# Router products with the gate's weights stationary, in four column strips of the array, and a transpose back

## Chip, core and metric

The kernel runs on one core of a Trainium2 chip. The metric is the device time of one execution in microseconds (us). Engines are called PE (TensorE, products), PEld (TensorE's loads of the stationary operand), DVE (VectorE), ACT (ScalarE), POOL (GpSimd) and SP (SyncE, which issues most DMAs).

## What is computed

A "macaron" layer over x of shape 8 x 1024 x 128 in fp32: half a mixture-of-experts FFN, a causal attention, and the same half FFN once more, each over a layer norm of x.

```python
x = x + 0.5 * ffn(layernorm(x))
x = x + attention(layernorm(x))        # rotary, causal, one head of 128
x = x + 0.5 * ffn(layernorm(x))

def ffn(x):                            # xt: tokens x 128; 16 experts of 64 units, top 4
    scores = sigmoid(xt @ gate_w.T)
    _, idx = top_k(scores + gate_b, 4)
    w = take_along_axis(scores, idx)
    w = 2.5 * w / sum(w)
    comb = zeros(T, 16).at[arange(T)[:, None], idx].add(w)
    for e in range(16):
        h = silu_and_mul(xt @ w13[e].T)
        y = y + comb[:, e:e+1] * (h @ w2[e].T)
    return y + silu_and_mul(xt @ w13_s.T) @ w2_s.T
```

The change concerns the first line of the FFN only: the product of the tokens with the gate, 128 x 16.

## The kernel before

Tokens are handled in groups of 512 (`W`), four tiles (`GT`) of 128. There are eight batches of two groups, and two FFN layers: 32 groups in all, in one list with a hand-made order in which layer 1 of a batch follows its layer 0 at a distance of four batches. Group p of the list is *period* p of the program. Its main work, on PE, is: one shared up product (`up_shared`, L254), then eight steps `up(k)`, each with a gate product (L264) and an up product (L265) of 128 x 512, then nine steps `down(k)` (L276). ACT makes the silu of each up step (L267), DVE the product with it (L269), POOL the product with the routing weight `cb` (L270).

All other work is hung between these steps. A period has the slots U0 to U8 (after `up_shared` and after each up step) and D0 to D8 (after each down step). `at(p, slot, f)` puts a function into a slot, and `run` calls those of a slot in the order in which they were put there. The engines' queues are in order and follow this program order; nothing is rescheduled afterwards (`manual_schedule`). In a slot the attention's functions come first, then those of `Heads`, then those of the router, then `add` and the statistics.

The router of group p is a chain of nine functions, most of them in period p-2:

- `norm_a` (U5), `norm_b` (D1): deviation and normed tokens `xn`
- `turn` (D4): four transposes on PE (L164), one copy by ACT (L165) into `hT`, 128 x 512, which has the features on the partitions
- `route` (D6): four products (L188), a tile of `hT` stationary (128 x 128), the gate `gw` (128 x 16) streaming, so that tokens come out on partitions
- `score` (D7): ACT's exponent of the logits in PSUM (L194)
- `top_a`, `top_b` (D8), then `top_c` (period p-1, U1): the top four and their weights on DVE (L198 to L226)
- `spread` (period p-1, U3): a transpose of the weights (L235), a copy (L237), one DMA out to DRAM and four DMAs that spread them over `cb`

Group 1 has slots of its own in period 0, and group 0 runs its chain at once, before period 0.

The attention puts up to three queries into a period. The first has its exponent in D0, its transposes in D3 and D5, and its `attend` (products with V, L395, and DVE's update of x, L399) in D7; the second has its exponent in D5, its transposes in D8 and in U0 of the next period; the third has its scores in D4 and its exponent in D7. Scores are L356, the exponent is L367, the transposes are L383, their copies L387 (ACT) or L389 (DVE).

PSUM has eight banks of 512 fp32. Banks 6 and 7 are shared by all small PE work and are handed out in turn by `other_bank()`: a user waits until the reader of the use before last is through.

In fp32, a product takes two instructions on PE, each with its own load; a transpose takes one. The program orders them as load, product, load, product.

Of the kernel before, what the change touches and what calls it, by code (L numbers as in the profile page):

```python
# [9 lines left out]
F32 = mybir.dt.float32  # L10
AF = mybir.ActivationFunctionType
# [4 lines left out]
P = 128  # L16
# [10 lines left out]
def kernel(  # L27
# [14 lines left out]
    nc = tc.nc  # L42

    B, S, D = x.shape
    E = gate_w.shape[1]
    I = w_sh_down.shape[0]
    NT = S // P
    GT = 4
# [7 lines left out]
    const = ctx.enter_context(tc.tile_pool(name="const", bufs=1))  # L56
    xpool = ctx.enter_context(tc.tile_pool(name="xpool", bufs=5))
    ln = ctx.enter_context(tc.tile_pool(name="ln", bufs=2))
    small = ctx.enter_context(tc.tile_pool(name="small", bufs=3))
# [8 lines left out]
    def bank(i, n=1):  # L68
        return psum[:, i * W : (i + n) * W]
# [3 lines left out]
    def other_bank():  # L73
        spare[0] += 1
        return bank(6 + spare[0] % 2)
# [4 lines left out]
    ident = const.tile([P, P], F32, name="ident")  # L80
# [16 lines left out]
    def load_x(b, g):  # L97
        if g == 0:
            xs[b] = xpool.tile([P, NT, D], F32, tag="x", name=f"x{b}")
        tiles = slice(g * GT, (g + 1) * GT)  # L100
        nc.sync.dma_start(
            out=xs[b][:, tiles, :], in_=x[b].rearrange("(t p) d -> p t d", p=P)[:, tiles, :]
        )

    load_x(0, 0)
    gw = const.tile([P, E], F32, name="gw")
    nc.scalar.dma_start(out=gw, in_=gate_w)
    gb = const.tile([P, E], F32, name="gb")
    nc.scalar.dma_start(out=gb, in_=gate_b.broadcast_to([P, E]))
    ws = const.tile([P, 2 * I], F32, name="ws")  # L110
# [24 lines left out]
    def stats(key, b, tiles):  # L135

        if key not in mvs:
            mvs[key] = small.tile([P, NT, 2], F32, tag="mv", name=f"mv_{key}", bufs=16)
        for t in tiles:
            st = small.tile([P, 6], F32, tag="st", name=f"st_{key}_{t}")  # L140
            nc.vector.bn_stats(st, xs[b][:, t, :])
            nc.vector.bn_aggr(mvs[key][:, t, :], st)
# [26 lines left out]
    class Group:  # L169
# [12 lines left out]
            self.hT = ln.tile([P, W], F32, tag="hT", name=f"hT_{self.nm}")  # L182
            transposed(self.key, self.g, self.xn, self.hT)

        def route(self):
            self.lg = other_bank()[:, : GT * E].rearrange("p (j e) -> p j e", e=E)
            for j in range(GT):
                nc.tensor.matmul(  # L188
                    self.lg[:, j, :], self.hT[:, j * P : (j + 1) * P], gw, start=True, stop=True
                )  # L190

        def score(self):
            self.sc = small.tile([P, GT, E], F32, tag="sc", name=f"sc_{self.nm}")
            nc.scalar.activation(self.sc, self.lg, AF.Exp, scale=-1.0)  # L194

        def top_a(self):

# [221 lines left out]
    def at(p, slot, *fs):  # L419
        jobs.setdefault((p, slot), []).extend(fs)  # L420
# [3 lines left out]
    def when(p, slot):  # L424
        return p * len(slots) + slots.index(slot)
# [6 lines left out]
    for p in range(3, 29):  # L432
        for n in range(2 if p in (15, 21) or (p % 2 == 0 and p != 26) else 3):
            if not queue:
# [4 lines left out]
            s, first, e, t0, t1, a = (  # L439
                ((p, "U7"), 4, (p, "D0"), (p, "D3"), (p, "D5"), (p, "D7")),  # L440
                ((p, "D2"), 2, (p, "D5"), (p, "D8"), (p + 1, "U0"), (p + 1, "U2")),
                ((p, "D4"), 4, (p, "D7"), (p + 1, "U3"), (p + 1, "U4"), (p + 1, "U5")),
            )[n]
# [10 lines left out]
    for b in range(B):  # L454
        h, st = heads[b], starts[b]
        ready = when(turn_of[0, b, 1] + 1, "U7")
        if b == 0:
            p0, p1 = st - 1, st - 1
            places = ("U8", "D0", "D2", "D3", "D5", "D6", "D7", "D8")
        else:  # L460
            p0, p1 = st - 2, st - 1
            places = ("D0", "D3", "D5", "D8", "U1", "U3", "U4", "U6")
# [13 lines left out]

    for p, gr in enumerate(groups):
        steps = (
            gr.norm_a, gr.norm_b, gr.turn, gr.route, gr.score, gr.top_a, gr.top_b, gr.top_c,
            gr.spread,  # L480
        )
        if p == 1:
            places = [(0, s) for s in ("U1", "U2", "U5", "U6", "D0", "D1", "D2", "D3", "D4")]
        else:
            places = [(p - 2, s) for s in ("U5", "D1", "D4", "D6", "D7", "D8", "D8")]
            places += [(p - 1, "U1"), (p - 1, "U3")]
        if p > 0:
            for f, place in zip(steps, places):
                at(*place, f)
        if gr.layer == 1:  # L490
            for t in range(gr.g * GT, (gr.g + 1) * GT):
                assert done[gr.b, t] < when(p - 2, "U5")

        at(p + 1, "U3", gr.add)
        if gr.layer == 0:
            t = gr.g * GT
            for s in ("U5", "U7"):
                at(p + 1, s, lambda b=gr.b, t=t: stats(f"a{b}", b, (t, t + 1)))
                t += 2


    for b in range(2, B):
        p = turn_of[0, b, 0]
# [17 lines left out]
    gr = groups[0]  # L521
# [1 line left out]
    gr.norm_a()  # L523
    gr.norm_b()
    gr.turn()
    gr.route()
    gr.score()
    gr.top_a()
    gr.top_b()
# [90 lines left out]
```

## Time and profile before

| what | value |
|---|---|
| time, median of 3 runs (lowest, highest) | 1028.06 us (1027.17, 1028.55) |
| the profiled execution's own time | 1027.84 us |
| its span, from the first to the last instruction | 1025.7 us |
| mean granted PE clock | 0.997 |
| ACT's exponent of the logits (L194), 32 of them | mean 223 ns |
| DVE's copy of yT (L279), 32 of them | mean 682 ns |

The profile is one execution, taken by the hardware profiler. A row of a group gives line, engine, operation, names (out <- in), shapes and count, then the busy time in us and the mean of one in ns, then the engine's idle time just before such instructions and what ended it. A row of the timeline gives start and length in us; "x4" stands for four instructions in a row, merged, so that its length runs from the start of the first to the end of the last. Products are pipelined and their ends are modelled, so what a product costs PE is read from one start to the next, not from its length.

### The profile page before, as it was taken

What the parts mean: (1) busy time and instruction counts of PE and PEld (TensorE: products, weight loads), DVE (VectorE), ACT (ScalarE), POOL (GpSimd) and SP (SyncE); (2) the same over time, 40 slices, a digit from 0 to 9 for tenths busy, and PEclk for the clock granted to TensorE, in tenths of its full rate; (3) what the DMA queues carried; (4) which work ended last, traced back from release to release, by engine and by line L of the source; (5) the groups of instructions that cost most, each with busy time, mean ns of one, the idle gap of its engine ahead of it and who ended that gap; (6) DMA issues with size and microseconds to landing.
All of it is one profiled execution on the core that took longest, in us unless ns stands there. A gap on an engine that the chain in (4) does not pass through costs nothing.

```text
span 1025.7 us, 11327 instructions
## 1 busy us (share of the span) xinstructions
PE 993.1 (97%) x3520; PEld 534.2 (52%) x3520; DVE 662.5 (65%) x2032; ACT 419.7 (41%) x734; POOL 451.9 (44%) x382
## 2 busy tenths in 40 slices
PE   5799999999999999999999999999999999999997
PEld 2344455554555455545555555555565555555543
DVE  3566877667775776667677665776657757665542
ACT  2233544443534454434444444443444444343321
POOL 1445734265425562345524464334643355322433
PEclk9999999999999999999999999999999999999999
DMA  5485431354214530345213451234412343124440
GB/s 143 110 173 105 84 67 32 69 104 84 46 39 94 115 81 6 81 94 114 61 23 84 94 114 43 43 82 94 94 42 57 69 94 83 48 58 94 94 93 21
DMA packets 56748, 80.20 MB, mean 78 GB/s; under 512 B 3504, under 2 KB 23280, under 8 KB 56560
## 3 DMA queue, kind: packets, MB, share of 16 engines
q1 hardware_dynamic: 55680, 78.36, 35.5%
q10 hardware_dynamic: 1008, 1.13, 0.3%
q8 instruction: 27, 0.44, 0.2%
q14 instruction: 33, 0.27, 0.1%
HBM read 74.24 MB, written 5.24 MB: 77 GB/s over the span
## 4 chain that ended last, share of the span: by engine, by line
PE 86%; DVE 7%; DMA 2%; issue 2%; ACT 2%; POOL 0%; SPq 0%; ACTq 0%; POOLq 0%; DVEq 0%
PE psum L276 23%; PE psum L265 18%; PE psum L264 17%; PE psum L356 6%; PE psum L395 6%; PE psum L383 3%; PE psum L323 3%; PE psum L188 3%; PE psum L164 2%; PE psum L254 2%; DVE hidT L269 1%; DMA cb<-cd 1%; PE psum L337 1%; DVE sel L220 1%; PE psum L284 1%
## 5 line engine op out<-in xcount | busy, mean ns | idle before, releaser
L270 POOL TENSOR_TENSOR hidT<-hidT,cb 128x512 f32<-128x512 f32 x256 | 324.0, 1270 | 545.2 <-DVE hidT L269 497.3
L265 PE MATMUL psum<-hT,wu 128*128 128x512 f32 x512 | 263.2, 596 | 4.4 <-DVE hidT L269 4.4
L264 PE MATMUL psum<-hT,wg 128*128 128x512 f32 x512 | 263.4, 596 | 0.0
L267 ACT ACTIVATE sg<-psum 128x512 f32<-128x512 f32 x256 | 152.7, 597 | 233.0 <-PE psum L264 217.5
L276 PE MATMUL psum<-hidT,wd 128*128 128x512 f32 x512 | 248.0, 598 | 0.0
L269 DVE TENSOR_TENSOR hidT<-psum,sg 128x512 f32<-128x512 f32 x256 | 175.2, 686 | 100.5 <-PE psum L265 98.4
L265 PEld LDWEIGHTS psum<-hT,wu 128*128 128x128 f32 x512 | 97.7, 191 | 128.2 <-issue 104.2
L276 PEld LDWEIGHTS psum<-hidT,wd 128*128 128x128 f32 x512 | 89.2, 191 | 69.0 <-issue 62.7
L264 PEld LDWEIGHTS psum<-hT,wg 128*128 128x128 f32 x512 | 89.4, 193 | 65.8 <-issue 62.8
L387 ACT COPY prT<-psum 128x512 f32<-128x512 f32 (+2 forms) x64 | 32.4, 506 | 158.6 <-PE psum L383 158.6
L395 PEld LDWEIGHTS psum<-v,prT 128*128 128x128 f32 x576 | 74.4, 192 | 30.6 <-issue 26.5
L395 PE MATMUL psum<-v,prT 128*128 128x128 f32 x576 | 74.6, 275 | 0.0
L356 PE MATMUL psum<-k,q 128*128 128x512 f32 (+2 forms) x192 | 72.4, 486 | 0.0
L399 DVE SCALAR_TENSOR_TENSOR x<-psum,rl,x 128x128 f32<-128x128 f32 x64 | 22.1, 346 | 77.1 <-PE psum L395 70.0
L155 DVE TENSOR_SCALAR xn_f<-x,mv_f,rs_f 128x128 f32<-128x128 f32 x128 | 65.6, 573 | 5.8 <-POOL rs_f L148 5.7
L383 PEld LDWEIGHTS psum<-ident,pr 128*128 128x128 f32 x288 | 36.8, 141 | 49.9 <-issue 42.9
L356 PEld LDWEIGHTS psum<-k,q 128*128 128x128 f32 x192 | 36.6, 190 | 45.8 <-issue 45.1
L362 DVE TENSOR_REDUCE top<-psum 128x1 f32<-128x128 f32 (+3 forms) x64 | 48.5, 758 | 2.2
L383 PE MATMUL psum<-ident,pr 128*128 128x128 f32 x288 | 47.4, 274 | 1.9 <-DVE x L287 1.9
L367 ACT ACTIVATE pr<-psum,top 128x128 f32<-128x128 f32 (+3 forms) x64 | 47.3, 743 | 0.3
L360 DVE TENSOR_TENSOR psum<-psum,causal 128x128 f32<-128x128 f32 x64 | 19.0, 296 | 42.4 <-PE psum L356 42.0
L256 ACT ACT_TABLE_LOAD x31 | 39.8, 1283 | 10.2 <-PE psum L254 10.1
(77 smaller groups left out, 1013.6 us busy)
## 6 DMA issues: line engine op xcount, KB each, us to landing
cb<-cd SPq DMA_DIRECT2D x128, 512.0 KB, 8.5
x<-in_x SPq DMA_DIRECT2D x16, 256.0 KB, 10.9
out_x<-x SPq DMA_DIRECT2D x16, 256.0 KB, 2.4
cd<-cT SPq DMA_DIRECT2D x32, 32.0 KB, 1.8
cs<-in_rope SPq DMA_DIRECT2D x1, 1024.0 KB, 12.4
wd<-in_w_down SPq DMA_DIRECT2D x1, 512.0 KB, 8.1
wg<-in_w_gate ACTq DMA_DIRECT2D x2, 256.0 KB, 7.5
wu<-in_w_up ACTq DMA_DIRECT2D x2, 256.0 KB, 6.4
```

Source lines behind the costliest of these rows:

```text
L155: nc.vector.tensor_scalar(xn[:, j, :], xs[b][:, t, :], mvs[key][:, t, 0:1], rstd[:, j : j + 1], ALU.subtract, ALU.mult,)
L264: nc.tensor.matmul(g_ps, wg[:, units], self.hT, start=True, stop=True)
L265: nc.tensor.matmul(u_ps, wu[:, units], self.hT, start=True, stop=True)
L267: nc.scalar.activation(sg, g_ps, AF.Silu)
L269: nc.vector.tensor_tensor(hid, u_ps, sg, ALU.mult)
L270: nc.gpsimd.tensor_tensor(hid, hid, self.cb[:, k, :], ALU.mult)
L276: nc.tensor.matmul(self.y, w, h, start=(k == 0), stop=(k == NP))
L356: nc.tensor.matmul(s[:, c:e], h.q[:, i * P : width], h.k[:, c:e], start=True, stop=True)
L362: nc.vector.tensor_reduce(top, s[:, :width], AX.X, ALU.max)
L367: nc.scalar.activation(self.pr[:, : self.width], self.s[:, : self.width], AF.Exp, bias=self.top, scale=SCALE, accum_out=self.h.rl[:, self. ...
L383: nc.tensor.transpose(tp[:, j, :], self.pr[:, (k + j) * P : (k + j + 1) * P], ident)
L395: nc.tensor.matmul(o, self.prT[:, j, :], self.h.v[:, j, :], start=(j == 0), stop=(j == i))
```

## The change

The gate's weights become the stationary operand. `gw` is widened from 16 to 32 columns (`SW`), with zeros in the columns from 16 on, and each of the four token tiles gets a product of its own with it, in its own strip of 32 columns of the array: tile j writes partitions 32 j to 32 j + 31 of one 128 x 128 piece of PSUM. The logits now have experts on the partitions and tokens on the columns. ACT copies this piece to SBUF (`lt`), PE transposes it, and the exponent reads the 16 valid columns of each strip from the transposed piece.

`route` thereby becomes two functions, and one slot is used differently: `route_a` (products and copy) stands in D5, `route_b` (the transpose) in D7, ahead of `score`, which stays in D7. In period 0, for group 1, they stand in U6 and U8. Group 0 calls them one after the other.

```diff
-    gw = const.tile([P, E], F32, name="gw")
-    nc.scalar.dma_start(out=gw, in_=gate_w)
+    SW = P // GT
+    gw = const.tile([P, SW], F32, name="gw")
+    nc.vector.memset(gw[:, E:], 0.0)
+    nc.scalar.dma_start(out=gw[:, :E], in_=gate_w)
...
-        def route(self):
-            self.lg = other_bank()[:, : GT * E].rearrange("p (j e) -> p j e", e=E)
+        def route_a(self):
+            lt = other_bank()[:, :P]
             for j in range(GT):
                 nc.tensor.matmul(
-                    self.lg[:, j, :], self.hT[:, j * P : (j + 1) * P], gw, start=True, stop=True
+                    lt[j * SW : (j + 1) * SW, :], gw, self.hT[:, j * P : (j + 1) * P],
+                    start=True, stop=True, tile_position=(0, j * SW),
                 )
+            self.lt = small.tile([P, P], F32, tag="lt", name=f"lt_{self.nm}", bufs=2)
+            nc.scalar.copy(self.lt, lt)
+
+        def route_b(self):
+            self.lg = other_bank()[:, :P]
+            nc.tensor.transpose(self.lg, self.lt, ident)
 
         def score(self):
             self.sc = small.tile([P, GT, E], F32, tag="sc", name=f"sc_{self.nm}")
-            nc.scalar.activation(self.sc, self.lg, AF.Exp, scale=-1.0)
+            lg = self.lg.rearrange("p (j e) -> p j e", e=SW)[:, :, :E]
+            nc.scalar.activation(self.sc, lg, AF.Exp, scale=-1.0)
...
-            gr.norm_a, gr.norm_b, gr.turn, gr.route, gr.score, gr.top_a, gr.top_b, gr.top_c,
-            gr.spread,
+            gr.norm_a, gr.norm_b, gr.turn, gr.route_a, gr.route_b, gr.score, gr.top_a, gr.top_b,
+            gr.top_c, gr.spread,
         )
         if p == 1:
-            places = [(0, s) for s in ("U1", "U2", "U5", "U6", "D0", "D1", "D2", "D3", "D4")]
+            places = [(0, s) for s in ("U1", "U2", "U5", "U6", "U8", "D0", "D1", "D2", "D3", "D4")]
         else:
-            places = [(p - 2, s) for s in ("U5", "D1", "D4", "D6", "D7", "D8", "D8")]
+            places = [(p - 2, s) for s in ("U5", "D1", "D4", "D5", "D7", "D7", "D8", "D8")]
             places += [(p - 1, "U1"), (p - 1, "U3")]
...
-    gr.route()
+    gr.route_a()
+    gr.route_b()
```

## Prediction

> **What bounds the kernel now.** I read the page first, from its top: busy shares, then the chain that ended last.
>
> ```profile
> span 1025.7 us, 11327 instructions
> PE 993.1 (97%) x3520; PEld 534.2 (52%) x3520; DVE 662.5 (65%) x2032; ACT 419.7 (41%) x734; POOL 451.9 (44%) x382
> ...
> PE 86%; DVE 7%; DMA 2%; issue 2%; ACT 2%; POOL 0%; SPq 0%; ACTq 0%; POOLq 0%; DVEq 0%
> PE psum L276 23%; PE psum L265 18%; PE psum L264 17%; PE psum L356 6%; PE psum L395 6%; PE psum L383 3%; PE psum L323 3%; PE psum L188 3%; PE psum L164 2%; PE psum L254 2%; DVE hidT L269 1%; DMA cb<-cd 1%; PE psum L337 1%; DVE sel L220 1%; PE psum L284 1%
> ```
>
> TensorE is the bound, and the router's line L188 is itself on the chain with 3% of the span, some 27 us. Busy time by stretch says whether that holds everywhere:
>
> ```profile
> 0.00:35.00 35.00, 19.18 (x43) 9.67 (x44) 15.13 (x62) 8.23 (x13) 10.87 (x22) 0.95 0.65 175
> 35.00:190.00 155.00, 151.13 (x488) 76.82 (x487) 110.31 (x360) 64.86 (x112) 78.38 (x65) 1.00 0.43 90
> 190.00:560.00 370.00, 366.46 (x1370) 202.44 (x1369) 249.98 (x782) 160.06 (x284) 162.71 (x133) 1.00 0.33 71
> 560.00:900.00 340.00, 336.70 (x1234) 184.11 (x1233) 225.53 (x672) 147.08 (x262) 156.22 (x128) 1.00 0.35 74
> 900.00:1025.00 125.00, 119.63 (x391) 61.17 (x389) 61.55 (x160) 39.45 (x66) 43.75 (x35) 1.00 0.32 70
> ```
>
> The second time in each row is the stretch, the third TensorE's busy time. From 35 us on it is 99% busy in the two middle rows. So what the change adds to or takes from TensorE's own stream goes into the time nearly one for one, 31 times; only the first group (before 35 us) is different. Next, the groups of instructions with shapes kept apart:
>
> ```profile
> L188 PEld LDWEIGHTS psum<-gw,hT 128*128 128x128 f32 x256 | 34.4, 196 | 15.8 <-issue 13.1 <-ACT pr L367 1.7 <-ACT hT L165 1.0
> ...
> L188 PE MATMUL psum<-gw,hT 128*128 128x16 f32 x256 | 31.7, 256 | 0.7 <-ACT hT L165 0.7
> ...
> L237 ACT COPY cT<-psum 64x128 f32<-64x128 f32 x32 | 8.3, 258 | 26.2 <-PE psum L235 25.8
> ```
>
> 256 in 32 groups is eight pairs of load and product a group: four token tiles in two passes each (fp32). The loads are 128 columns, the products stream only 16. What a group really costs is in the timeline of one steady group (start, length):
>
> ```profile
> 227.07 0.27 PE L383 MATMUL psum<-ident,pr 128*128 128x128 f32 x1
> ...
> 227.18 1.02 PE L276 MATMUL psum<-hidT,wd 128*128 128x512 f32 x2
> ...
> 228.04 0.60 PE L164 MATMUL psum<-ident,xn_f 128*128 128x128 f32 x4
> ...
> 228.48 1.88 PE L276 MATMUL psum<-hidT,wd 128*128 128x512 f32 x4
> 228.68 0.58 ACT L165 COPY hT<-psum 128x512 f32<-128x512 f32 x1 [1.03 <-PE psum L164]
> ...
> 230.20 0.96 PE L188 MATMUL psum<-gw,hT 128*128 128x16 f32 x8
> 230.20 0.86 PEld L188 LDWEIGHTS psum<-gw,hT 128*128 128x128 f32 x7 [0.24 <-issue]
> ...
> 231.01 1.11 PE L276 MATMUL psum<-hidT,wd 128*128 128x512 f32 x2
> ...
> 231.95 0.38 PE L395 MATMUL psum<-v,prT 128*128 128x128 f32 x2
> ```
>
> Start to start, four L276 passes take 230.20 - 228.48 = 1.72, or 0.43 each. From the first L188 to the L395 are 1.75, of which two L276 passes are 0.86: a group of router products costs **0.89 us** of stream. The loads set it: seven in 0.86 with 0.19 for the last is (0.86 - 0.19)/6 = 0.11 from one to the next, which 16 streamed columns cannot hide.
>
> **What the Trainium skill says.** "TensorEngine Tiling (Array Packing)", Performance Considerations, names this very swap (small streamed side made stationary, four column strips) with up to 4x. "TensorE: Matmul & The Clock Gate", Part 3, gives 2.38x for three column strips at 512 columns, and says that products start and end strictly in program order. The first page again, Key Properties: changing the tiling mode drains TensorE. No instruction in this trace runs in a strip, so none of the three can be checked here. The second page's section on LDWEIGHTS makes a load proportional to columns at 1.2 per ns: 0.107 for 128, and the 0.11 above agrees.
>
> **The change, part by part.** *Removed*: 0.89 us of stream in each of 31 steady groups.
>
> *Added, the strips (route_a).* Still eight pairs, now with loads of 32 columns (0.11 x 32/128 = 0.03 estimated from the row) and 128 streamed columns (0.11 a pass: 227.07 to 227.18 is one such product). Three readings. Nothing overlaps: 8 x 0.11 = 0.88. Everything overlaps and only loads pace it: 8 x 0.03 + 0.11 = 0.35. In between, which I take: starts are in order, and the two passes of one strip follow each other in the program, so pass two waits 0.11 for its own strip, while pass one of the next strip starts right after it, a load later. That is four waits of 0.11, three loads of 0.03 and the last 0.11: **0.64**.
>
> *Added, two switches of mode.* A product's recorded length exceeds its start-to-start time by 596 - 430 = 166 ns (modelled ends), which is the tail that a drain would expose. Below, nothing (a switch is free). Above, two tails and the loads that then can't be made ahead: 0.33 + 0.11 + 0.03 = 0.47. I take the two tails alone, **0.33**, since the skill states the drain but not that loads are held too.
>
> *Added, the transpose back (route_b).* One load and one product: **0.11** by the same L383 row.
>
> Sum: 0.64 + 0.33 + 0.11 = 1.08 against 0.89: +0.19 a group, 31 x 0.19 = +5.9 us.
>
> *ScalarE*: a copy of 128x128, 0.26 by the L237 row, 32 times, 8.3 us on an engine 41% busy. It stands in slot D5 behind the exponent of the second query (and its sum), at most about 1.3 us in all, and its reader comes two down products (1.72) and an attend later, so it is covered; uncovered it would cost its 0.26 a group, 8 us. Behind it in ScalarE's queue is only the third query's exponent, which waits for VectorE anyway. The exponent of the logits stays in D7 behind that one, but starts about 1 us later than now, since route_b ends D7. Its reader top_a stands in D8 behind the copy of yT, which cannot start before D8's product ends, 0.86 later; the exponent needs some 0.17 + 0.22, so nothing moves.
>
> *Moved: route_a one slot up, D6 to D5.* It now needs hT one product earlier. The copy ends at 228.68 + 0.58 = 229.26; D5's product has issued at 228.48 + 0.86 = 229.34. Margin 0.08, and a wake-up took 0.05 in the first group (copy over at 9.29, L188 at 9.34). It fits barely, and a drain would hide a miss; a miss of 0.1 would be 3 us in all. No DMA moves. PSUM: the two shared banks alternate; route_a finds its bank freed by hT's copy or an older one, route_b by its own data or older. The next query's transposes in D8 now wait for the x update of the attend instead of for the exponent; a product of 0.86 lies between, so zero.
>
> *Start.* The first group is exposed and at half clock: eight L188 from 9.34, the exponent at 11.27, 1.93 in all. New: strips 2 x 0.64 = 1.3, tail 0.17, copy 0.26, transpose with tail 0.4, semaphores 0.1: 2.2, so +0.3 (bounds -0.2 to +0.8). The memset of the padding (0.07 on VectorE) lies before the load of gw; the ACT queue would carry a delay to gb, which lands at 6.67, but hT's copy that follows waits until 8.70. Zero.
>
> **Total**: +6.2 us on the profiled execution's own 1027.84 (span 1025.7 plus about 2.1 around it), which stands 0.2 below the median 1028.06. **1034 us.**
>
> **Rivals.** (A, the forecast) strips overlap in pairs, the switches cost about two tails. With switches from 0.20 to 0.47: +0.06 to +0.33 a group, +2 to +10.5 us; 1030 to 1038.5. For it: in-order starts and the two passes; against it: the drain is only stated. Chance 0.35.
> (B) fp32 strips don't overlap: 0.88 + 0.33 + 0.11 = 1.32, +0.43 a group, +13.3 and 0.8 at the start: 1042 (1032 with free switches, 1046.5 with dear ones). For it: this fp32 stream already runs at 0.43 per 512 columns in each of two passes, so reading may be the limit. Against: the 2.38x of the skill. Chance 0.22.
> (C, the other side) the switch costs nearly nothing. Place: the two edges of route_a; price 0 to 0.05 for both; it decides as soon as strips and switches are together below 0.89 - 0.11 = 0.78. With pairs: 0.64 + 0.11 + 0.03 = 0.78, -0.11 a group, -3.4 + 0.3: 1024.7. With full overlap 0.35 + 0.11 + 0.03 = 0.49, -0.40 a group, -12.4: 1015.5. For it: other changes of what the array does (transposes between products) show no bubble here, 0.11 for a lone L383. Against: those stay on the whole array. Chance 0.34.
> (D) a wash: switches of about 0.1 with paired strips, 1026 to 1030. Chance 0.09.
>
> **How the numbers follow.** A measurement of this kernel tells 0.2%, 2 us, from no change. Faster is C, 0.34; same is D, 0.09; slower is A and B, 0.57. The range leaves out the bottom of C (about 0.08) and the top of B (about 0.06): 1020 to 1044. As both signs carry weight: A's own range is 1030 to 1038.5.
>
> **What would show it.** In the new timeline: the starts of the eight strip products (gaps alternating 0.11 and 0.03 for pairs, all 0.11 for B, all 0.03 for full overlap); the time from the last L276 before them to the first, over 0.43 by the drain, and from the last strip product to the next L276; 0.11 for the transpose back. A wait of TensorE for hT at D5, or of VectorE for the exponent at D8, would be new and would prove my zeros wrong. The forecast falls if the switches show no bubble, or if the strips start 0.03 apart.

## Result: 0.8% faster, and the profile after

| | before | after |
|---|---|---|
| median of 5 runs (lowest, highest) | 1028.06 us (1027.17, 1028.96) | 1019.8 us (1018.37, 1020.34) |
| the profiled execution's own time | 1027.84 us | 1019.8 us |
| its span | 1025.7 us | 1018.0 us |

The ratio is 0.9917, 95% interval 0.9905 to 0.9929. The forecast was 1034, slower; 1020 was the low end of its range. What happened is nearest to rival C, but not for the reason that C gave.

The page of the changed kernel has the same bound, and the chain of waits shows the router's line (now L192) no longer among those of 2% or 3%:

```profile
span 1018.0 us, 11428 instructions
PE 985.1 (97%) x3552; PEld 511.5 (50%) x3552; DVE 664.4 (65%) x2033; ACT 427.1 (42%) x766; POOL 452.1 (44%) x382
...
PE psum L288 24%; PE psum L277 18%; PE psum L276 18%; PE psum L368 6%; PE psum L407 6%; PE psum L395 3%; PE psum L335 3%; PE psum L167 2%; PE psum L266 2%; DVE hidT L281 2%; DVE sel L232 1%; PE psum L349 1%; PE psum L192 1%; PE psum L296 1%; DMA cb<-cd 1%
```

Thirty-two products more (the transposes back), and yet 8 us less of busy TensorE. The groups of instructions with shapes apart say which: the router's products were busy for 31.7 us and are now for 13.9, and the transpose back and the copy cost what the rows of before had promised.

```profile
L192 PE MATMUL psum<-hT,gw 128*32 128x128 f32 x256 | 13.9, 289 | 0.7 <-ACT hT L168 0.7
L201 PE MATMUL psum<-ident,lt 128*128 128x128 f32 x32 | 8.9, 279 | 0.4 <-ACT lt L197 0.4
L197 ACT COPY lt<-psum 128x128 f32<-128x128 f32 x32 | 8.5, 266 | 7.2 <-PE psum L192 7.1
```

The timeline of TensorE for the same group whose timeline stands in the prediction (start, length):

```profile
227.27 1.02 PE L288 MATMUL psum<-hidT,wd 128*128 128x512 f32 x2
228.22 0.42 PE L192 MATMUL psum<-hT,gw 128*32 128x128 f32 x8
228.58 1.98 PE L288 MATMUL psum<-hidT,wd 128*128 128x512 f32 x4
230.40 0.39 PE L407 MATMUL psum<-v,prT 128*128 128x128 f32 x2
230.62 0.27 PE L201 MATMUL psum<-ident,lt 128*128 128x128 f32 x1
230.73 1.02 PE L288 MATMUL psum<-shared,wsd 128*128 128x512 f32 x2
```

Two passes of L288 should hold the stream for 0.86; the first strip product starts 0.95 after them, so **0.09** is lost at the entry. The next L288 comes 0.36 after the first strip product. Its four passes take 1.82 in place of 4 x 0.43 = 1.72, so another **0.10** is lost after the exit. The transpose holds the stream for 0.11. Together 0.09 + 0.36 + 0.10 + 0.11 = **0.66** against 0.89 before: -0.23 in each of 31 groups, -7.1 us. The trace shows this gain arriving in the time: the first product of `up_shared` comes 0.76 us earlier than before in period 4 and 6.78 us earlier in period 30, which is 0.23 a period.

Why is anything lost after the exit? TensorE's loads around the visit say it, the first row from before, the other two from after:

```profile
229.77 0.19 PEld L188 LDWEIGHTS psum<-gw,hT 128*128 128x128 f32 x1 [0.24 <-ACT pr L367]
```

```profile
228.22 0.16 PEld L192 LDWEIGHTS psum<-hT,gw 128*32 128x32 f32 x8 [0.76 <-ACT hT L168]
228.58 0.30 PEld L288 LDWEIGHTS psum<-hidT,wd 128*128 128x128 f32 x2 [0.20 <-issue]
```

Before, the first load stood 0.43 ahead of its product (229.77 and 230.20). After, the first load of the strips and the first load behind them start with their products (228.22 and 228.58), so nothing covers them. The eight loads of the strips are all recorded within 0.16.

The first group gains too, as its timeline shows:

```profile
9.26 0.65 PE L192 MATMUL psum<-hT,gw 128*32 128x128 f32 x8 [0.67 <-ACT hT L168]
...
10.81 0.23 ACT L206 ACTIVATE sc<-psum 128x64 f32<-128x64 f32 x1 [0.56 <-PE psum L201]
```

```profile
9.34 1.89 PE L188 MATMUL psum<-gw,hT 128*128 128x16 f32 x8 [0.67 <-ACT hT L165]
...
11.27 0.22 ACT L194 ACTIVATE sc<-psum 128x64 f32<-128x64 f32 x1 [1.98 <-PE psum L188]
```

(First after, then before.) From the products to the exponent 1.55 in place of 1.93: -0.4. The two parts come to 7.5, and the span fell by 7.7, but the sum does not close so well in detail. The last store of x is issued 6.8 us earlier (first before, then after):

```profile
1021.45 0.38 SPq L289 DMA_DIRECT2D out_x<-x  x1
```

```profile
1014.66 0.38 SPq L301 DMA_DIRECT2D out_x<-x  x1
```

The other 0.9 lies behind that issue, where the change does nothing; its cause is open. And by period 4 the parts promise 0.4 + 5 x 0.23 = 1.6, of which only 0.76 is there. In this execution the mean granted clock from 20 to 36 us was 0.79, and 0.89 before, which may be the reason; no run separates it.

How the eight products stand in those 0.36 is seen by cutting the groups off in time. Of those that overlap 228.20 to 228.30, and then 228.20 to 228.40:

```profile
L192 PE MATMUL psum<-hT,gw 128*32 128x128 f32 x4 | 0.3, 297 | 0.0
```

```profile
L192 PE MATMUL psum<-hT,gw 128*32 128x128 f32 x8 | 0.4, 285 | 0.0
```

Four start at once, the other four about a pass later: neither the pairs of the prediction nor a single file. Either all four first passes run side by side, or the strips go two by two with both their passes. And are the 0.09 and 0.10 the price of switching the mode? The experiments ask this.

### The profile page after: what moved, and what is told of

Its sections match the earlier page's. It is cut to its first block, busy times and chain, and to the rows that moved or that the text cites. A ratio compares the mean times of both kernels' runs of the same rounds, so it can differ in the third digit from the quotient of the medians.

```text
span 1018.0 us, 11428 instructions
## 1 busy us (share of the span) xinstructions
PE 985.1 (97%) x3552; PEld 511.5 (50%) x3552; DVE 664.4 (65%) x2033; ACT 427.1 (42%) x766; POOL 452.1 (44%) x382
## 4 chain that ended last, share of the span: by engine, by line
PE 85%; DVE 9%; issue 2%; ACT 2%; DMA 1%; POOL 0%; SPq 0%; ACTq 0%; POOLq 0%; DVEq 0%
PE psum L288 24%; PE psum L277 18%; PE psum L276 18%; PE psum L368 6%; PE psum L407 6%; PE psum L395 3%; PE psum L335 3%; PE psum L167 2%; PE psum L266 2%; DVE hidT L281 2%; DVE sel L232 1%; PE psum L349 1%; PE psum L192 1%; PE psum L296 1%; DMA cb<-cd 1%
## 5 line engine op out<-in xcount | busy, mean ns | idle before, releaser
L288 PE MATMUL psum<-hidT,wd 128*128 128x512 f32 x512 | 246.5, 599 | 0.0
L288 PEld LDWEIGHTS psum<-hidT,wd 128*128 128x128 f32 x512 | 89.9, 190 | 80.7 <-issue 74.4
```

Source lines behind the costliest of these rows:

```text
L288: nc.tensor.matmul(self.y, w, h, start=(k == 0), stop=(k == NP))
```

## Experiments

**One strip for all four tiles**: does the gain come from the strips or from the short loads?

```diff
+                at_ = j * SW if self.n == 0 else 0
                 nc.tensor.matmul(
-                    lt[j * SW : (j + 1) * SW, :], gw, self.hT[:, j * P : (j + 1) * P],
-                    start=True, stop=True, tile_position=(0, j * SW),
+                    lt[at_ : at_ + SW, :], gw, self.hT[:, j * P : (j + 1) * P],
+                    start=True, stop=True, tile_position=(0, at_),
```

> The changed kernel with all four token tiles sent through the first strip of 32 columns (the four products write the same 32 partitions one after the other, so that the logits of three of the four tiles are lost; group 0 keeps its four strips). Loads, products, copy, transpose and both switches of mode stay; only the spreading over strips goes. In the changed kernel a visit of the strips costs 0.55 us of TensorE's stream beyond the product before it (0.09 at the entry, 0.16 from first to last start, 0.20 to the next L288, 0.10 until its second pass). Theory S (the gain comes from strips running side by side): the eight products go to 0.11 apart, first to last start 7 x 0.11 = 0.77 instead of 0.16, +0.61 in each of 31 groups: +19 us, 1038.7. Theory L (the gain comes from the short loads of 32 columns, strips bring nothing): no change, 1019.8, starts some 0.01 apart in fours as now.

Measured 1040.45 us, ratio to the kernel before 1.011 (1.0093 to 1.0127): +20.7 over the changed kernel. TensorE's timeline in one group:

```profile
233.20 1.02 PE L289 MATMUL psum<-hidT,wd 128*128 128x512 f32 x2
234.16 1.06 PE L193 MATMUL psum<-hT,gw 128*32 128x128 f32 x8
235.15 1.99 PE L289 MATMUL psum<-hidT,wd 128*128 128x512 f32 x4
236.97 0.27 PE L408 MATMUL psum<-v,prT 128*128 128x128 f32 x1
```

From the first strip product to the next L289 is 0.99 in place of 0.36; the 0.10 at the entry (0.96 - 0.86) and after the exit (1.82 - 1.72) are unchanged within rounding. So the spreading over strips is worth 0.63 a group; without it the change would lose 1.1%.

**The whole array**: the same products with the weights padded to 128 columns, no strip mode.

```diff
-    gw = const.tile([P, SW], F32, name="gw")
+    gw = const.tile([P, P], F32, name="gw")
...
-                    lt[j * SW : (j + 1) * SW, :], gw, self.hT[:, j * P : (j + 1) * P],
-                    start=True, stop=True, tile_position=(0, j * SW),
+                    lt, gw, self.hT[:, j * P : (j + 1) * P], start=True, stop=True
```

> The changed kernel with the gate's weights padded to 128 columns and the four products on the whole array, each writing the same 128 x 128 piece (logits of three of the four tiles are lost). No strip mode at all, so no switch of mode; copy and transpose stay. Theory D (the 0.09 before the first strip product and the 0.20 after the last one, of which 0.11 is streaming, are a drain at each switch of mode): the entry falls back to 0.43 after the L288 product before, the eight products are 0.11 apart, and the next L288 follows 0.11 after the last: 0.88 in all, +0.33 over the 0.55 of the changed kernel, 31 x 0.33 = +10 us, 1030; and some 9 us below e_one_strip. Theory E (the edges are the wait for hT or the gate's own loads, not the mode): the same 0.09 and 0.20 stand here too, about 1.15 a group, 1038, level with e_one_strip.

Measured 1033.3 us, ratio 1.0044 (1.003 to 1.0058), 7 below the single strip. One group:

```profile
229.60 1.02 PE L287 MATMUL psum<-hidT,wd 128*128 128x512 f32 x2
229.80 0.59 ACT L168 COPY hT<-psum 128x512 f32<-128x512 f32 x1 [1.03 <-PE psum L167]
...
230.44 0.97 PEld L192 LDWEIGHTS psum<-hT,gw 128*128 128x128 f32 x8 [0.64 <-ACT hT L168]
230.46 1.14 PE L192 MATMUL psum<-hT,gw 128*128 128x128 f32 x8
...
231.44 1.45 PE L287 MATMUL psum<-hidT,wd 128*128 128x512 f32 x3
```

The entry is 230.46 - 229.60 = 0.86: nothing is lost there once the mode stays, and nothing after the exit. The eight hold 0.98, not 0.88: the first load waits for hT (over at 230.39, recorded start 230.44) and isn't made ahead, 0.08 in such groups. Where the attention's transposes in D5 give hT time, the eight hold 0.90 (196.74 - 195.84):

```profile
195.63 0.38 PE L394 MATMUL psum<-ident,pr 128*128 128x128 f32 x2
195.84 1.06 PE L192 MATMUL psum<-hT,gw 128*128 128x128 f32 x8
196.74 1.45 PE L287 MATMUL psum<-hidT,wd 128*128 128x512 f32 x3
```

That wait in 16 of the 31 groups (1.3 us) and a longer start (2.43 us from the first product to the transpose back, 1.04 in the changed kernel) make most of the 3 us by which the run is above its expectation. In strip mode it doesn't show: the entry loses 0.09 right behind D5's product, and no more and no less behind transposes (two strips, below).

**Halved products**: who starts before whom?

```diff
-                nc.tensor.matmul(
-                    lt[j * SW : (j + 1) * SW, :], gw, self.hT[:, j * P : (j + 1) * P],
-                    start=True, stop=True, tile_position=(0, j * SW),
-                )
+                for a, b in ((0, 96), (96, P)):
+                    nc.tensor.matmul(
+                        lt[j * SW : (j + 1) * SW, a:b], gw, self.hT[:, j * P + a : j * P + b],
+                        start=True, stop=True, tile_position=(0, j * SW),
+                    )
```

> The changed kernel with each strip's product cut in two, tokens 0 to 95 and 96 to 127, strip by strip in the program, so that the widths tell which product starts when. In the program each strip then has four products: 96, 96 (its two passes), 32, 32. Theory Q (each strip has a line of its own; the first pass of a later strip overtakes the waiting second pass of an earlier one): the starts come as four of 96, four of 96, four of 32, four of 32, from first to last start 0.08 + 0.08 + 0.03 = 0.19 and a little, no change of the whole within 2 us: 1020. Theory P (products start in program order, two passes of a strip one after the other): 96, 96, 32, 32, 96, 96, and so on, the first pass of the next strip beside the last of the strip before, 4 x 0.22 less 3 x 0.03 = 0.79 from first to last: +0.6 a group, +19 us. Theory B (four products at a time, whatever their strip, the two passes of one strip side by side): the first four starts are 96, 96, 32, 32.

Measured 1021.05 us, ratio 0.992 (0.9903 to 0.9937), so no change from the changed kernel. The products that overlap 228.94 to 229.00, then 228.94 to 229.13, then 228.94 to 229.25:

```profile
L193 PE MATMUL psum<-hT,gw 128*32 128x96 f32 x4 | 0.3, 270 | 0.0
```

```profile
L193 PE MATMUL psum<-hT,gw 128*32 128x96 f32 x8 | 0.4, 258 | 0.0
```

```profile
L193 PE MATMUL psum<-hT,gw 128*32 128x96 f32 x8 | 0.4, 258 | 0.0
L193 PE MATMUL psum<-hT,gw 128*32 128x32 f32 x8 | 0.3, 194 | 0.0
```

All eight products of 96 have started before any of 32, although strip 0's narrow product stands ahead of strip 1's wide one in the program. Theory Q holds, P and B fall: a later strip overtakes an earlier one that is waiting.

A rival would be that the instructions reach TensorE in another order than the one written. The gaps speak against it: within the first four starts, a strip comes 7 ns after the one before in the changed kernel, which has four instructions (two loads, two products) to a strip, and 13 ns after it here, with eight. In an order by rounds, two instructions would lie between the starts in both kernels.

**Two strips for four**, the same edit as for one strip with `j // 2 * SW` for the position.

> The changed kernel with two strips for four: token tiles 0 and 1 go through strip 0, tiles 2 and 3 through strip 1, so that the logits of two tiles are lost (group 0 keeps its four strips). In the program the order is four passes of strip 0, then four of strip 1. If strips have lines of their own, the two lines run side by side: starts in pairs 0.01 apart, pairs 0.11 apart, from first to last 3 x 0.11 = 0.34 instead of 0.16, +0.18 a group, +5.5 us, 1025.3, between the changed kernel and the one with a single strip (1040.5). If a line could look only one product ahead in the program (my reading in the prediction, only neighbours overlap): 7 starts 0.11 apart less one overlap, 0.66, +0.5 a group, +16 us, 1035.5.

Measured 1025.88 us, ratio 0.9977 (0.9966 to 0.9987): +6.1. One group:

```profile
193.74 0.38 PE L396 MATMUL psum<-ident,pr 128*128 128x128 f32 x2
194.05 0.64 PE L193 MATMUL psum<-hT,gw 128*32 128x128 f32 x8
194.62 1.98 PE L289 MATMUL psum<-hidT,wd 128*128 128x512 f32 x4
```

0.57 for eight products; four strips take 0.36, one takes 0.99. With four passes to a strip in place of two, the line of the busiest strip sets the time: 0.21 for two passes more. In the trace the eight starts come in four pairs, 13 ns apart within a pair, and from pair to pair 0.13 us the first time and 0.11 then; two passes of one strip are never side by side. The two transposes ahead hold 0.22, so the entry loses its 0.09 here too, where hT has been ready for longer.

**The products twice in one visit**, the first time into the unread neighbour columns of the bank.

```diff
-            lt = other_bank()[:, :P]
-            for j in range(GT):
+            both = other_bank()
+            lt = both[:, :P]
+            for to in (both[:, P : 2 * P], lt):
+                for j in range(GT):
...
```

> The changed kernel with the strips' four products made twice in the same visit (the first time into the next 128 columns of the bank, which nobody reads). Sixteen pairs of load and product for eight, the same two switches of mode. If a visit costs 0.31 for the switches (0.09 to drain, the first load, 0.09 to drain, 0.11 for the first load after) and the rest for the four passes side by side, each strip now has four passes for two: +0.22 a group, 31 x 0.22 = +6.8 us, 1026.6. If the switch price belonged to the products (each set brings it again): +0.5 a group, +16 us, 1035.

Measured 1026.86 us, ratio 0.9985 (0.9978 to 0.9992): +7.1. The price of the switches belongs to the visit and not to the products.

**The visit cut in two**, by giving `route_a` an argument:

```diff
-            for j in range(GT):
+            for j in (2 * half, 2 * half + 1):
...
-            places = [(p - 2, s) for s in ("U5", "D1", "D4", "D5", "D7", "D7", "D8", "D8")]
+            places = [(p - 2, s) for s in ("U5", "D1", "D4", "D5", "D6", "D7", "D7", "D8", "D8")]
```

> The changed kernel with the visit cut in two: strips 0 and 1 in slot D5, strips 2 and 3 in slot D6, a whole down product between them, the copy after the second. As many loads and products as in the changed kernel, twice as many switches of mode. If the mode switch is what costs 0.09 at the entry and 0.09 + 0.11 at the exit: a visit of two strips is 0.09 + 0.13 + 0.20 + 0.10 = 0.53 of stream, two are 1.06 against 0.55, +0.51 a group, +16 us, 1035.5. If switches cost nothing and the passes set the price: two visits of two passes are 0.24 + 0.24 against 0.26, +0.22 a group, +7 us, 1026.6.

Measured 1035.86 us, ratio 1.0074 (1.0057 to 1.0091): +16.1. One group:

```profile
230.70 1.02 PE L292 MATMUL psum<-hidT,wd 128*128 128x512 f32 x2
231.65 0.41 PE L194 MATMUL psum<-hT,gw 128*32 128x128 f32 x4
231.99 1.13 PE L292 MATMUL psum<-hidT,wd 128*128 128x512 f32 x2
233.05 0.41 PE L194 MATMUL psum<-hT,gw 128*32 128x128 f32 x4
233.39 1.12 PE L292 MATMUL psum<-hidT,wd 128*128 128x512 f32 x2
```

Twice the products cost 7, twice the visits of half the products 16. Both runs have two more rounds of passes in each of 31 groups, some 7 us; the remaining 9 us, 0.29 a group, are the second pair of switches: the same 0.09 at the entry and about 0.2 around the exit.

**The slot**: products back in D6.

```diff
-            places = [(p - 2, s) for s in ("U5", "D1", "D4", "D5", "D7", "D7", "D8", "D8")]
+            places = [(p - 2, s) for s in ("U5", "D1", "D4", "D6", "D7", "D7", "D8", "D8")]
```

> The changed kernel with the strips' products and their copy in slot D6, where the products stood before, and not in D5. Theory: the slot brings nothing, since neither hT in D5 nor lt in D7 is waited for: entry 0.52 after the product before as now, time within 1 us of 1019.8. Rival: the earlier slot is part of the gain (a wait of the transpose back for lt in D7, at most 0.3 a group): up to +9 us, 1029.

Measured 1018.93 us, ratio 0.9903 (0.9887 to 0.9918), an interval that overlaps that of the change. One group:

```profile
225.98 1.88 PE L288 MATMUL psum<-hidT,wd 128*128 128x512 f32 x4
227.79 0.42 PE L192 MATMUL psum<-hT,gw 128*32 128x128 f32 x8
```

The slot is no part of the gain. And the entry loses 227.79 - 225.98 - 1.72 = 0.09 here as well, with hT ready one product earlier, so the loss is no wait for hT.

## Why the prediction was wrong, step by step

- *What is removed*, 0.89 a group, and *that TensorE's stream goes into the time one for one*: right. From period 4 on, each period gains the 0.23 that its group gains.
- *The strips*, 0.64: **the step that failed.** "starts are in order, and the two passes of one strip follow each other in the program, so pass two waits 0.11 for its own strip, while pass one of the next strip starts right after it". That pass two waits for its own strip is right (0.11 apart with one strip), the order of starts isn't: a waiting pass holds back only its own strip. All first passes run side by side, then all second ones, 0.16 from first to last start and 0.11 for the last, 0.27. The reading in which everything overlaps (0.35) was the nearest, and still priced the starts too high: they come some 0.01 apart, since the short loads overlap as well (eight within 0.16). The order came from "TensorE: Matmul & The Clock Gate", Part 3; for products in different strips the halved products contradict it, and the measurement decides.
- *The two switches*, 0.33: about right at 0.29 (entry 0.09, and 0.20 from the end of the last pass into the next product). The composition was off: the tail of 166 ns was taken from modelled lengths, what is lost is some 0.09 at each edge, while the first load of 128 columns after the exit is exposed, which I had left to the upper bound. With the drain of "TensorEngine Tiling (Array Packing)", Key Properties, this agrees: the whole array shows no such loss, and a second visit brings it again. That it is a draining, and not another part of the switch, the runs don't separate. The whole array also changed the width of the weights together with the mode. A narrow stationary operand alone brought no loss where the traces have one, in the transpose of the weights (L235, 64 columns: started 142.09, the next product 142.20); products with 32 columns outside the strips were not run.
- *The transpose back* (0.11) and *the copy on ScalarE* (266 ns, covered): right. *hT in D5*: a miss was hidden by the switch, as written; without strip mode it costs 0.08 in about half of the groups.
- *The start*, +0.3: it was -0.4, by the same mis-sized strips. From their first start to the transpose back are 1.04 us, where the forecast's terms add up to 1.8.
- *Rival C* had the sign, but its reason, a free switch, was wrong: switches cost 0.29. With 0.27 in the sum's first term, the forecast's own prices give 0.27 + 0.33 + 0.11 = 0.71, -0.18 a group or 5.6 us faster, before the start.

## What to carry to other kernels

Small products on a busy TensorE are worth putting into column strips when enough of them come in one visit: with products of 128 columns, a visit cost 0.29 us of stream at its edges here whatever was in it, 0.03 to 0.05 for its first load and the strips' staggered starts, and 0.11 for each pass of the fullest strip. Count the passes of the fullest strip, not the products, and don't cut a visit in two. The price of a mode switch is read at its edges, from start to start against the known time of the product before.

## What the runs showed of the hardware

- Products in different column strips are not held to program order: eight of 96 columns started before the first of 32 that stood ahead of six of them. Within a strip the passes stayed in order. So what is said ahead of the prediction, that the engines' queues are in order, does not hold for starts in different strips.
- fp32 products in two passes overlap over strips: four times two passes of 128 columns held 0.36 us up to the next whole-array product, one strip alone 0.99.
- A change between the whole array and strips of 32 lost 0.09 us at the entry in each of the 30 groups of the changed kernel from 47 us on, after products of 512 columns and after transposes alike. At the exit it lost 0.09 before the next product and, with a first load that nothing covered, 0.10 after it.
- The starts of neighbouring strips lay 7 ns apart with four instructions to a strip, and 13 ns with eight.
